# A four-layer graph network kernel: merged weights between the steps of layer 2, node weights of layer 3 summed by TensorE, one square root per pair's layer norm

## The chip, the cores and the metric

The kernel runs on one core of a Trainium2 chip, alone. The metric is the device time of one execution in microseconds (us). Each kernel was run several times, with a mean granted TensorE clock of 0.95 of full speed. In the views of the profile PE is TensorE's products, PEld its weight loads, DVE VectorE, ACT ScalarE, POOL GpSimd and SP the engine that issues loads. They count instructions, and an fp32 product is two. In the code `sb.tile` makes the tiles that engines work from and `ps.tile` those in PSUM, into which products are written; `bufs` is how many buffers a tag has.

## The reference

Eight graphs of 2048 nodes with 64 features go through four residual layers, each `x = x + layer(relu(layer_norm(x)))`. The change touches the last two:

```python
# layer 2, v = relu(layer_norm(x)) with node 0 replaced by an intervention value
for _ in range(3):
    effects = jnp.einsum('nm,bmd->bnd', adj_matrix, v)
    h = jnp.concatenate([v, effects], axis=-1)
    h = jax.nn.relu(jnp.einsum('bnk,dk->bnd', h, W1) + b1)
    v = jnp.einsum('bnk,dk->bnd', h, W2) + b2

# layer 3, x = relu(layer_norm(x)); embedding is (2048, 16), weight (16, 3, 64, 64), bias (16, 64)
w = jnp.einsum('nd,dkio->nkio', embedding, weight)
b = jnp.einsum('nd,do->no', embedding, bias)
As = [eye, A, 2.0 * (A @ A) - eye]
x_g = jnp.einsum('knm,bmc->bnkc', jnp.stack(As, 0), x)
out = jnp.einsum('bnki,nkio->bno', x_g, w) + b
```

## The kernel before

Everything is fp32. `x` lies transposed, one tile per pair of graphs, with (graph, feature) on the 128 partitions and the nodes along the free axis. A pair is worked off in four chunks of 512 nodes (`CW`); four pairs run one after another. A multiplication by the adjacency ("spread") of one chunk is sixteen products of 128 rows.

```python
def layer_norm_relu(dst, src, ps, sb, c, ...):      # one chunk
    mm(mean, avg, src[:, s], start=True, stop=True)
    nc.vector.tensor_sub(xc, src[:, s], mean)
    nc.scalar.activation(q, xc, AF.Square)
    mm(var, avg, q, start=True, stop=True)
    nc.scalar.activation(q, var, AF.Sqrt, bias=eps)
    nc.vector.reciprocal(q, q)                      # 128 x 512, of which two rows differ
    nc.vector.scalar_tensor_tensor(dst[:, s], xc, 0.0, q, op0=OP.max, op1=OP.mult)

for p in range(NP):                                  # a pair of graphs
    nc.sync.dma_start(out=xp, in_=x2_dram[p])
    ...                                              # layer norm and transposes into vN
    for step in range(3):                            # layer 2
        for c in range(NCW):
            pe = spread(vN, c)
            nc.vector.tensor_copy(ef, pe)
            mm(ph, W1v, v[:, cols(c)], start=True, stop=False)
            mm(ph, W1e, ef, start=False, stop=True)
            nc.scalar.activation(hh, ph, AF.Relu, bias=b1)
            mm(pv, W2, hh, start=True, stop=True)
            ...                                      # last: add to xp; else v = pv + b2, four transposes
    ...                                              # layer 3: layer norm, transposes, first spread y1
    for c in range(NCW):
        ...                                          # second spread y2
        for k in range(4):                           # node tiles of 128
            nc.tensor.transpose(px, xp[:, ns], ident)
            for h in range(2):                       # graphs
                for kk, src in enumerate((z[:, ns], y1[:, ns], y2[:, k * P : (k + 1) * P])):
                    for w in range(2):
                        mm(uf[:, cols(w)], src[half(h), :], W3[half(h), kk, cols(w)], ...)
                nc.vector.tensor_tensor(pr, u, emb[:, i, :, None].to_broadcast([P, D3, F]), op=OP.mult)
                nc.vector.tensor_reduce(oo, pr.rearrange("p d o -> p o d"), AX.X, OP.add)
                nc.vector.tensor_add(oo, oo, bias3[:, i, :])
                nc.vector.tensor_add(oo, oo, px[:, half(h)])
```

## Time and profile before

| | before |
|---|---|
| time, median of 4 runs | 6355.57 us (6353.63 to 6357.78) |
| busy, TensorE / VectorE / ScalarE | 86% / 66% / 40% of the span |
| layers 2 and 3 begin at | about 4212 us |
| one pair, layers 2 and 3 | 516 us |

### The profile page before, as it was taken

The numbers are of one execution on the slowest core, as the hardware profiler recorded it, in microseconds if no ns is written. First come the engines' busy times: TensorE is split into PE (matmuls) and PEld (weight loads), VectorE is DVE, ScalarE is ACT, GpSimd is POOL, SyncE is SP. The second block draws the span as 40 slices with busy tenths as digits, with TensorE's granted clock in tenths as the row PEclk, the third lists the DMA queues.
The fourth block names the chain that finished last, engine by engine and source line by source line (L and its number), as shares of the span: only waits on it lengthen the run. The fifth ranks groups of instructions, "written<-read, shape, count | busy, mean of one in ns | idle before, by whom it ended". The sixth has DMA issues, their size and how long they took to land.

```text
span 6355.8 us, 40025 instructions
## 1 busy us (share of the span) xinstructions
PE 5490.6 (86%) x15272; PEld 2629.2 (41%) x15272; DVE 4224.4 (66%) x4499; ACT 2559.2 (40%) x2656; POOL 87.0 (1%) x134
## 2 busy tenths in 40 slices
PE   5985888888888888888778888849999999999999
PEld 2433333333333333333356666634343343444444
DVE  5016999999999999999599999941153144135035
ACT  1003767676767676766266666620000000000000
POOL 0000000000000000000000000000000000000000
PEclk7996999999999999999699999979999999999999
DMA  0110000000000000000000000030000000000000
GB/s 27 66 50 0 0 0 1 0 0 0 0 0 0 0 1 0 0 0 0 1 36 31 6 30 25 5 128 0 0 5 8 0 4 10 0 2 12 0 0 7
DMA packets 44832, 73.36 MB, mean 12 GB/s; under 512 B 25296, under 2 KB 29520, under 8 KB 39760
## 3 DMA queue, kind: packets, MB, share of 16 engines
q1 hardware_dynamic: 43488, 62.41, 3.0%
q10 hardware_dynamic: 1152, 8.39, 0.3%
q8 instruction: 120, 1.97, 0.1%
q14 instruction: 72, 0.59, 0.0%
HBM read 62.40 MB, written 8.39 MB: 11 GB/s over the span
## 4 chain that ended last, share of the span: by engine, by line
DVE 45%; PE 44%; issue 6%; ACT 5%; DMA 1%; SPq 0%; ACTq 0%; DVEq 0%
PE pe L536 17%; DVE hd L315 9%; DVE hd L333 9%; DVE hd L332 9%; PE u L600 9%; PE acc L204 4%; DVE z L432 3%; DVE q L102 2%; DVE z L442 2%; PE acc L335 2%; DVE pT L456 2%; DVE z L430 2%; PE var L100 1%; PE o L459 1%; PE tp L110 1%
## 5 line engine op out<-in xcount | busy, mean ns | idle before, releaser
L335 PE MATMUL acc<-hd,sel 128*128 128x512 f32 x2048 | 1044.0, 634 | 319.1 <-DVE hd L333 318.8
L330 PE MATMUL cr<-coefT,pick 128*128 128x512 f32 x2048 | 957.7, 592 | 0.0
L314 ACT ACTIVATE hd<-h,AGm 128x1024 f32<-128x1024 f32 x512 | 586.8, 1149 | 520.0 <-PE acc L335 487.0
L335 PEld LDWEIGHTS acc<-hd,sel 128*128 128x128 f32 x2048 | 359.4, 195 | 998.8 <-DVE hd L333 737.6
L536 PE MATMUL pe<-aT,vN 128*128 128x512 f32 x1536 | 682.1, 594 | 0.0
L315 DVE SCALAR_TENSOR_TENSOR hd<-th,hd 128x1024 f32<-128x1024 f32 x512 | 651.4, 1275 | 44.5 <-ACT hd L314 31.8
L332 DVE SCALAR_TENSOR_TENSOR hd<-hd,AG,th 128x1024 f32<-128x1024 f32 x512 | 658.6, 1291 | 0.0
L459 PE MATMUL o<-pT,hN 128*128 128x256 f32 x2048 | 529.7, 395 | 114.5 <-DVE pT L456 110.9
L333 DVE TENSOR_TENSOR hd<-hd,cr 128x1024 f32<-128x1024 f32 x512 | 620.6, 1212 | 4.8 <-PE cr L330 3.9
L313 ACT ACTIVATE th<-hg,AE 128x1024 f32<-128x1024 f32 x512 | 576.6, 1135 | 42.7 <-DVE hd L332 27.9
L330 PEld LDWEIGHTS cr<-coefT,pick 128*128 128x128 f32 x2048 | 388.2, 190 | 492.4 <-issue 484.5
L331 ACT ACTIVATE th<-th 128x1024 f32<-128x1024 f32 x512 | 532.0, 1042 | 82.3 <-DVE th L316 82.0
L459 PEld LDWEIGHTS o<-pT,hN 128*128 128x128 f32 x2048 | 369.2, 192 | 211.0 <-DVE pT L456 146.2
L600 PE MATMUL u<-W,y 64*128 64x512 f32 x1024 | 450.3, 590 | 0.0
L536 PEld LDWEIGHTS pe<-aT,vN 128*128 128x128 f32 x1536 | 290.5, 191 | 353.5 <-issue 353.5
L98 ACT ACTIVATE q<-xc 128x512 f32<-128x512 f32 x64 | 40.3, 630 | 902.7 <-DVE xc L96 902.7
L556 DVE COPY ef<-pe 128x512 f32<-128x512 f32 x48 | 33.2, 692 | 548.9 <-PE pe L536 548.9
L316 DVE TENSOR_SCALAR th<-hd,AG 128x1024 f32<-128x1024 f32 x512 | 380.4, 746 | 0.6
L454 PE MATMUL tp<-ident,z 128*128 128x128 f32 x2048 | 301.9, 276 | 45.3 <-ACT pT L456 35.6
L561 ACT ACTIVATE hh<-ph,b 128x512 f32<-128x512 f32 x48 | 33.0, 687 | 707.7 <-PE ph L559 707.7
L440 ACT ACTIVATE z<-z,mx 128x2048 f32<-128x2048 f32 x128 | 256.8, 2006 | 122.9 <-DVE mx L435 122.2
L454 PEld LDWEIGHTS tp<-ident,z 128*128 128x128 f32 x2048 | 244.9, 141 | 133.2 <-ACT pT L456 86.3
(198 smaller groups left out, 5849.9 us busy)
## 6 DMA issues: line engine op xcount, KB each, us to landing
at<-in_adjT SPq DMA_DIRECT2D x16, 1024.0 KB, 5.1
neg<-in_adj SPq DMA_DIRECT2D x16, 1024.0 KB, 4.9
aT<-in_adjT SPq DMA_DIRECT2D x8, 1024.0 KB, 19.9
aT<-in_adjT ACTq DMA_DIRECT2D x8, 1024.0 KB, 19.5
x<-in_xT SPq DMA_DIRECT2D x16, 256.0 KB, 5.7
x_dram<-x SPq DMA_DIRECT2D x32, 128.0 KB, 1.9
xp<-x_dram SPq DMA_DIRECT2D x4, 1024.0 KB, 4.8
out<-ot SPq DMA_DIRECT2D x32, 128.0 KB, 1.9
```

The lines of the kernel that those rows point to most:

```text
L313: nc.scalar.activation(th, hg, AF.Tanh, bias=AE[:, b, ep : ep + 1], scale=0.5)
L314: nc.scalar.activation(hd, h2, AF.Identity, bias=AGm[:, b, ep : ep + 1], scale=0.5)
L315: nc.vector.scalar_tensor_tensor(hd, th, 1.0, hd, op0=OP.add, op1=OP.mult)
L330: mm(cr[:, cols(k)], pick, coefT[:, p, c0 + k * CW : c0 + (k + 1) * CW], start=True, stop=True)
L331: nc.scalar.activation(th, th, AF.Exp)
L332: nc.vector.scalar_tensor_tensor(hd, hd, AG1[:, b, ep : ep + 1], th, op0=OP.add, op1=OP.max)
L333: nc.vector.tensor_mul(hd, hd, cr)
L335: mm(acc[:, cols(k)], sel[b2], hd[:, cols(k)], start=b2 == 0 and ep == 0, stop=b2 == 1 and ep == 31,)
L454: nc.tensor.transpose(tp[:, w, k, :], zs[k][:, m * P : (m + 1) * P], ident)
L459: mm(o, hN[:, m, p, :], pT[:, w, :], start=m == 0, stop=m == NT - 1)
L536: mm(pe, vN[:, m, :], aT[m][:, cols(c)], start=m == 0, stop=m == NT - 1)
L600: mm(uf[:, cols(w)], src[half(h), :], W3[half(h), kk, cols(w)], start=kk == 0, stop=kk == 2,)
```

## The change

Three independent ideas, to take work from TensorE's small products and from VectorE:

- **Merged weights.** Between two steps of layer 2, `W2` and the next step's `W1` are multiplied once beforehand (`V12`, `E12`, and the biases they bring). The copy of the spread, two products and an activation per chunk disappear, and the transposes become products with `E12` that leave the result transposed.
- **One square root per layer norm.** The variances of all four chunks go into one tile, one chunk per 32 partitions, so that one `Sqrt` and one reciprocal serve the pair in place of four. A product with `spr` spreads the result out again.
- **Node weights on the partitions.** The products of layer 3 put (two embedding dimensions, 64 outputs) on the partitions and the nodes on the free axis. VectorE multiplies by the embedding, loaded in broadcast, in one instruction per graph, and TensorE sums over the dimensions with `sum2`, two stacked identities. The reductions over 16 strided elements disappear.

The core of the diff, cut (new biases, loads and tile shapes left out):

```diff
+    def layer_norm_pair(dst, src):
+        for c in range(NCW):
+            mm(pxc, cen, src[:, s], start=True, stop=True)
+            nc.scalar.activation(q, pxc, AF.Square)
+            nc.vector.tensor_scalar_max(dst[:, s], pxc, 0.0)
+            mm(var[32 * c : 32 * c + 32, :], avr, q, start=True, stop=True)
+        nc.scalar.activation(rs, var, AF.Sqrt, bias=eps)
+        nc.vector.reciprocal(rs, rs)
+        for c in range(NCW):
+            mm(pb, spr[qd, :], rs[qd, :], start=True, stop=True)
+            nc.vector.tensor_mul(dst[:, s], dst[:, s], pb)
...
-                pe = spread(vN, c)
-                nc.vector.tensor_copy(ef, pe)
-                mm(ph, W1v, v[:, cols(c)], start=True, stop=False)
-                mm(ph, W1e, ef, start=False, stop=True)
...
+                mm(pe, V12 if step else W1v, v[:, s], start=True, stop=False)
+                spread(pe, uO, c, False, True)
+                nc.scalar.activation(v[:, s], pe, AF.Relu, bias=b12 if step else b1)
+                if step < 2:
+                    sent(c, E12, False)      # four products, then a VectorE add of cbc
...
+            for dp in range(DP):             # 8 steps of two embedding dimensions
+                em = sb.tile([P, CW], FP, tag="em", name="em", bufs=3)
+                ...                          # two loads of one row, read 64 times each
+                for kk, src in enumerate((z[:, s], y1[:, s], y2)):
+                    for h in range(2):
+                        mm(u[h], W3[half(h), kk, dp * P : (dp + 1) * P], src[half(h), :], ...)
+                for h in range(2):
+                    nc.vector.scalar_tensor_tensor(
+                        pr[h], u[h], bias3[:, dp : dp + 1], em, op0=OP.add, op1=OP.mult)
+                for h in range(2):
+                    mm(pout[half(h), :], sum2, pr[h], start=dp == 0, stop=dp == DP - 1)
+            nc.vector.tensor_add(xo, pout, xp[:, s])
```

## The prediction

> **What bounds the kernel now.** I read the page's busy shares first, then the chain of work that ended last in order of time, then the groups by shape and the timeline of layers 2 and 3. The change touches nothing before 4212 us, where layer 1 ends, so only the last third matters. The groups from 4150 us on carry these lines (busy us, mean ns, idle before):
>
> ```profile
> L536 PE MATMUL pe<-aT,vN 128*128 128x512 f32 x1536 | 682.1, 594 | 0.0
> L600 PE MATMUL u<-W,y 64*128 64x512 f32 x1024 | 450.3, 590 | 0.0
> L607 DVE TENSOR_REDUCE ot<-pr 128x64 f32<-128x1024 f32 x128 | 243.2, 1900 | 4.3
> L605 DVE TENSOR_TENSOR pr<-u,emb 128x1024 f32<-128x1024 f32 x128 | 156.3, 1221 | 153.2 <-PE u L600 153.2
> L102 DVE RECIPROCAL q<-q 128x512 f32<-128x512 f32 x32 | 107.3, 3353 | 82.2 <-ACT q L101 82.2
> ```
>
> An fp32 product is two instructions: 1536 is 2 x 4 pairs x 3 steps x 64. TensorE hardly waits (third column); VectorE waits for u. So layer 3's VectorE work (1221 + 1900 + 225 + 221 = 3567 ns per u, 32 per pair, 114 us of a pair's 516) lies beside TensorE and its removal frees nothing. The chain in order of time gives one pair's length and the cost of a u block:
>
> ```profile
> 5348.88 9.44 PE pe L536 x22
> ...
> 5363.57 12.02 PE pe L536 x28
> 5380.84 12.02 PE pe L536 x28
> ...
> 5671.80 8.89 PE u L600 x24
> 5680.69 13.93 PE pe L536 x32
> ...
> 5865.81 9.44 PE pe L536 x22
> ```
>
> A pair lasts 5865.3 - 5348.9 = 516 us after correction for the different start. A 16-tile spread (32 instructions) runs one instruction per 0.43 us, 13.73 us; a chunk of a step that is not the last takes 17.33 us (5380.84 - 5363.57, and so on), of the last 16.75. So 3.6 or 3.0 us per chunk are small products and waits. A u block of one node tile takes 9.15 us for 24 instructions, less than 24 x 0.43 = 10.3. TensorE's timeline says why:
>
> ```profile
> 5141.19 0.69 PE L600 MATMUL u<-W,z 64*128 64x512 f32 x1
> 5141.61 0.59 PE L600 MATMUL u<-W,y 64*128 64x512 f32 x1
> 5141.72 0.59 PE L600 MATMUL u<-W,z 64*128 64x512 f32 x1
> 5142.04 0.59 PE L600 MATMUL u<-W,y 64*128 64x512 f32 x1
> 5142.15 0.59 PE L600 MATMUL u<-W,z 64*128 64x512 f32 x1
> ```
>
> Here the last four products of one graph (partitions 0 to 63) run beside the first four of the other (64 to 127): two 64-row streams, each at 0.43 us. Today that happens only where h changes, 4 of 24 instructions.
>
> The layer norms are the only long idle time of TensorE. Before layer 2 the timeline goes from the end of u at 5315.9 to undisturbed spreading at 5348.7, with 10 spread instructions (4.3 us) done inside: 28.6 us lost. Before layer 3, from the end of spreading at 5546.9 to 5580.7, less 6.1 us of early u and spread and 3.0 us of the chunk's own products: 24.7 us lost. Four reciprocals in each, 13.4 us, are the largest piece. The matmuls in there often take twice as long (a pair of instructions 1.92 us in place of 1.02).
>
> **What the Trainium skill says.** "TensorEngine Tiling (Array Packing)", Key Properties: different tiles run in parallel, and a change of tiling mode drains the engine. The trace agrees with both: the interleaved starts above; and from u through the 128-row transpose px back to u about 0.35 us are lost over the 0.43 grid. The same page, PSUM Bottleneck, says that tiling does not speed up evacuation; that is what my estimate of layer 3 turns on. "TensorE: Matmul & The Clock Gate", Part 1, has a half-rate clock after an idle window of about 3.4 us and full rate after as long a busy one; the doubled durations inside the layer norms agree. The same page, Part 3, says matmuls start strictly in order; here z starts before y instructions that stand ahead of it in the program, so the trace differs and I go by the trace.
>
> **The change, part by part.**
>
> *Merged weights (layer 2).* A chunk loses the copy of pe, the product with W1e, W2 and its activation, and four transposes. It keeps one product with V12 (0.86), the spread (13.73), and gains four 128-wide products with E12. The similar four with W_ind in layer 0 took 1.05 to 1.49 us, I take 1.2. In the built order the next chunk's V12 product (0.86) stands between the spread and those four, and they need Relu: about 0.2 + 0.69 + 0.06 = 0.95, so 0.1 is left as a wait. Sum 15.9 against 17.33: 1.4 x 8 chunks = 11.5 us a pair. The last step's chunk: 0.86 + 13.73 + W2 0.86 + 0.15 = 15.6 against 16.75: 4.6 us. Together 16 a pair, 64 in all.
>
> *One sqrt per layer norm.* Before layer 3: four centring and four variance products, interleaved with Square, about 8 us from the last spread; sqrt and reciprocal 0.2 + 0.69 + 3.35 + 0.1 = 4.3; then four products that copy the scale out, two PSUM buffers, against VectorE multiplies of 0.69: 4 to 6 us, half clock after 4 us of idleness; four transposes and a copy 1.5. About 19 lost, against 24.7: 5 to 7 us a pair, 26 in all. The reciprocals save 10 us, but the four chunks no longer overlap and all end behind one barrier. Before layer 2 two things eat that up. xp has one buffer, and in the old kernel its last reader was a transpose some 9 us before u ended, so its load (5 us) was hidden. Now the last reader is the final addition to xo, after the last product: 0.9 + 0.1 + 4.8 = 6 us with TensorE idle and then slow. And the sixteen W1e products (5 us) come before the first spread. I get 6 + 9 (partly at half clock) + 4.4 + 10 = 29.5 against 28.6: nothing won at three pair changes; 5 us for the first pair, whose load was exposed already. The start of layers 2 and 3 loses the wait for the late bias load (TensorE waited until 4271.5, xp landed at 4283.6): 9 us.
>
> *Node weights on the partitions (layer 3).* A chunk had 4 x 9.15 = 36.6 us of u. Now it has 8 steps of six 64-row products, alternating between the halves, and two sum2 products over 128 rows. Alternating, the six take 6 x 0.86 / 2 = 2.6 us by the interleaving above. Then a new chain sets the step: the second half's u is complete 0.17 us after its last pass; VectorE's addition and multiplication is of the form of xp<-pv,b2c,xp, 750 ns; handovers 0.1; only then can the second sum2 product (0.86) run, the first being done by about that time (its own start also waits for VectorE). With 0.1 for exposed weight loads and 0.2 to 0.3 for mode changes, a step is 2.6 + 0.17 + 0.75 + 0.1 + 0.86 + 0.3 = 4.8 us. The built order puts only one product of the next step ahead of the sums, counted in the six. 8 x 4.8 = 38.4, plus 1.3 for the chunk's first extra product, the wait for xo and the transposes: 39.7 against 36.6, 3.1 x 16 chunks = 50 us more. VectorE (1.5 us a step) and the em loads (256 KB a step against 1 MB in 4.8 us, three buffers ahead) keep up. So the part that takes the most work off VectorE slows the path.
>
> Sum: 6356.6 - 64 - 26 - 5 + 3 - 9 + 50 = 6306; I put 6302, since the last step's estimate of waits is on the cautious side.
>
> **Rivals.**
> *No overlap of the 64-row streams in the new order:* the six products take 5.15 us; the waits then partly hide, a step is about 6.9 us, 57 a chunk: +330, 6600. Against it speaks the interleaving; for it, that today's runs are of four of one kind, and that the new order switches rows every two instructions.
> *The em loads become the bound:* each is one row read 64 times and written to 64 partitions. If a step's two took over 5 us, steps would follow them: at 6 us, 8 x 1.2 x 16 = +150, 6450. A 128 KB transfer lands in 1.9 us in this trace, so I give it one in ten.
> *VectorE was the real bound and the step is shorter:* if the sums of the two halves (different columns of the array) overlap and the wait for VectorE hides, a step is 4 us, -100 more, 6200. The last dependence (u complete, 0.75, sum 0.86) doesn't allow it as the order stands: 2.6 + 1.0 + 0.86 is a floor of 4.45.
> *Clock:* with fewer and longer gaps the layer norms may run more at half clock: up to +3 us each, +24.
>
> **Range and chances.** Layer 2's gain is read off measured chunks (55 to 72); the norms and the start could give 20 to 60; layer 3 lies between +5 (steps of 4.45) and +100 (5.2), with a tail to +330. That makes 6235 to 6400. Faster by 2% is below 6229 and needs everything at its best: 0.07. Slower by 2% is above 6484 and needs one of the first two rivals: 0.13.
>
> **What would show it right or wrong.** Right: chunks of layer 2 some 15.9 us apart; u products in alternating starts and eight groups of about 4.8 us per chunk, sum2 products waiting for pr from VectorE; one 3.35 us reciprocal per norm with TensorE idle beside it; TensorE waiting for the DMA of xp at three pair changes; VectorE's busy time down by about 350 us (63 a pair in layer 3, 19 in the norms, 5 in layer 2) with no gain from the first of these. Wrong: u products one after another 0.43 us apart throughout (first rival), pr waiting for em (second), or steps below 4.4 us.

## More of the kernel before

VectorE's 66% hides two different regimes: it is busy in layers 0 and 1, which the change does not touch, and waits for TensorE afterwards. So the last third is read by itself. The next lines are the view of busy time by stretches of the kernel before, for one pair. The stretches are, in order: the steps of layer 2; the layer norm before layer 3; the first spread of layer 3; its second spread with the node weights; the change to the next pair. The columns are start and end, length, then busy us and instructions of TensorE, its weight loads, VectorE, ScalarE and GpSimd, then the granted TensorE clock, DMA share and GB/s.

```profile
5348.70:5546.90 198.20, 198.20 (x475) 84.27 (x474) 15.39 (x22) 13.64 (x20) 0.00 (x0) 1.00 0.00 0
5546.90:5580.70 33.80, 22.06 (x58) 9.11 (x57) 19.65 (x14) 7.71 (x12) 0.00 (x0) 0.90 0.00 0
5580.70:5647.50 66.80, 66.76 (x168) 29.67 (x167) 2.77 (x4) 2.93 (x5) 0.00 (x0) 1.00 0.00 0
5647.50:5832.00 184.50, 184.50 (x490) 82.70 (x489) 112.18 (x129) 0.00 (x0) 0.00 (x0) 1.00 0.04 10
5832.00:5864.90 32.90, 20.55 (x38) 8.56 (x37) 21.61 (x17) 7.03 (x11) 0.00 (x0) 0.69 0.04 8
```

In three of the five stretches TensorE is busy throughout. In the fourth VectorE works 112 of 184 us without holding anything up. TensorE idles only in the two norms, where its clock also falls, to 0.90 and 0.69.

## The result, and the profile after

| | before | after |
|---|---|---|
| median of 4 runs | 6355.57 us | 6304.95 us (6301.44 to 6308.38) |
| ratio | | 0.9921, 95% interval 0.9907 to 0.9935 |
| busy, TensorE / VectorE | 5490.6 / 4224.4 us | 5482.1 / 3879.8 us |
| one pair | 516.2 us | 506.6 us |

A ratio is the mean time of one kernel's runs over that of the other's of the same rounds, so it is not quite the ratio of the medians quoted beside it. Differences between two changed kernels below are differences of such ratios to the kernel before, times 6354 us; the interval of one ratio is 8 to 11 us either way.

VectorE lost 345 us of work and the kernel gained 51. The same stretches of the kernel after, in the same view and columns:

```profile
4808.10:4995.40 187.30, 187.30 (x479) 85.05 (x479) 8.48 (x12) 7.56 (x11) 0.00 (x0) 1.00 0.00 0
4995.40:5019.30 23.90, 18.97 (x45) 7.15 (x44) 9.35 (x10) 5.52 (x9) 0.00 (x0) 0.77 0.00 1
5019.30:5091.90 72.60, 72.57 (x179) 31.96 (x177) 2.77 (x4) 2.93 (x5) 0.00 (x0) 0.98 0.00 0
5091.90:5284.90 193.00, 192.93 (x619) 65.99 (x618) 52.64 (x72) 1.75 (x3) 0.00 (x0) 1.00 0.17 47
5284.90:5314.70 29.80, 19.23 (x61) 9.43 (x62) 11.69 (x14) 3.66 (x6) 0.00 (x0) 0.77 0.19 53
```

The boundaries are not quite comparable, because some work of a stretch runs ahead inside the one before it. Before, 4.3 us of layer 2's spreading and 1.8 us of layer 3's second part ran ahead, and 3.0 us of products of layer 2's last chunk ran late; after, 0.9 us of layer 3's second part ran ahead and 1.1 us of layer 2 late. With those put back:

| stretch of a pair | before | after | difference | predicted |
|---|---|---|---|---|
| layer 2 | 205.5 | 188.4 | -17.1 | -16 |
| norm before layer 3 and first spread | 95.8 | 94.5 | -1.3 | -5 to -7 |
| layer 3, second part | 186.3 | 193.9 | +7.6 | +12.4 |
| norm at the pair change | 28.6 | 29.8 | +1.2 | +0.9 |
| sum | 516.2 | 506.6 | -9.6 | |

The two other pair changes in the same trace lost 31.5 and 32.2 us, 2.9 and 3.6 more than before. The first pair starts spreading at 4299.7 in place of 4312.8 (with what ran ahead put back), 13.1 us earlier (predicted 14). The first three rows four times, the three pair changes and the start make -43.2 + 7.7 - 13.1 = -48.6; the two traces differ by 50.9, and the 2.3 between them were not followed.

Three of the groups by shape of the kernel after, from 4150 us on, answer to those shown of before (columns: busy us, mean ns, then the idle time ahead with its releasers):

```profile
L660 PE MATMUL u<-y,W 64*128 64x512 f32 x1024 | 351.2, 601 | 0.0
...
L666 DVE SCALAR_TENSOR_TENSOR pr<-u,bias,em 128x512 f32<-128x512 f32 x256 | 191.2, 751 | 386.8 <-PE u L660 367.1 <-DMA em<-in_embT 9.3
...
L582 DVE RECIPROCAL rs<-rs 128x512 f32<-128x512 f32 x8 | 26.8, 3353 | 9.2 <-ACT rs L581 9.2
```

The 1024 instructions that read `y1` and `y2` keep TensorE busy for 351 us in place of 450, though each lasts as long, 601 ns against 590: more of them run side by side. (A group's busy time does not see pairs with another group: the 512 instructions that read `z` went from 247 to 266 us. The step below is the surer measure: twelve u instructions in 2.78 us, where 12 x 0.43 = 5.2 would be one after another.) VectorE waits for u, not for the loads of `em` (9.3 us in all). Eight reciprocals stand where there were 32. The timeline of one step of layer 3 after shows what fills its 4.69 us; the brackets give the idle time ahead and what ended it:

```profile
5206.86 1.59 DVE L666 SCALAR_TENSOR_TENSOR pr<-u,bias,em 128x512 f32<-128x512 f32 x2 [3.09 <-PE u L660]
...
5207.66 1.91 PE L670 MATMUL pout<-pr,sum 128*64 128x512 f32 x4
5208.50 0.19 PEld L670 LDWEIGHTS pout<-pr,sum 128*64 128x64 f32 x2 [0.65 <-DVE pr L666]
...
5209.51 0.69 PE L660 MATMUL u<-z,W 64*128 64x512 f32 x1
```

VectorE makes both `pr` one after the other, from 5206.86 to 5208.45. The weights of the second sum load at 5208.50, as soon as the second `pr` is there. The two sums write different columns of the array and could run together, yet they take 1.91 us, nearly two products of 0.86 in a row. VectorE works 1.59 of the 4.69 us: it is in the chain, and is not the bound.

TensorE's timeline of the norm before layer 3 after, from the end of the one reciprocal to the first spreading:

```profile
5008.21 1.87 PE L586 MATMUL pb<-rs,spr 32*128 32x512 f32 x4 [4.16 <-DVE rs L582]
5010.85 2.67 PE L586 MATMUL pb<-rs,spr 32*128 32x512 f32 x4 [0.77 <-DVE z L587]
5013.45 1.97 PE L110 MATMUL tp<-ident,z 128*128 128x128 f32 x8
5015.35 2.07 PE L660 MATMUL u<-z,W 64*128 64x512 f32 x2
5017.35 1.97 PE L110 MATMUL tp<-ident,z 128*128 128x128 f32 x8
5019.11 3.38 PE L592 MATMUL pe<-aT,zN 128*128 128x512 f32 x4
```

After 4.16 us of idleness these pieces take about twice their usual time: the two u instructions 2.07 us, where two such instructions in m_hout take 1.05, and four spread instructions 3.38 where 4 x 0.43 = 1.7 is usual. The granted clock from 5013.45 to 5019.31 is 0.50. And all sixteen transposes stand ahead of the first spread, since the four chunks of the norm end together.

### The profile page after: what moved, and what is told of

It reads as the page before. It is cut to its first block, busy times and chain, and to the rows that moved or that the text cites. A ratio compares the mean times of both kernels' runs of the same rounds, so it can differ in the third digit from the quotient of the medians.

```text
span 6304.9 us, 41599 instructions
## 1 busy us (share of the span) xinstructions
PE 5482.1 (87%) x15856; PEld 2569.3 (41%) x15856; DVE 3879.8 (62%) x4224; ACT 2519.8 (40%) x2600; POOL 87.0 (1%) x134
## 5 line engine op out<-in xcount | busy, mean ns | idle before, releaser
L592 PE MATMUL pe<-aT,uN 128*128 128x512 f32 x1536 | 667.1, 593 | 0.0
L592 PEld LDWEIGHTS pe<-aT,uN 128*128 128x128 f32 x1536 | 289.9, 190 | 351.5 <-issue 351.5
L666 DVE SCALAR_TENSOR_TENSOR pr<-u,bias,em 128x512 f32<-128x512 f32 x256 | 191.2, 751 | 386.8 <-PE u L660 367.1
L660 PE MATMUL u<-y,W 64*128 64x512 f32 x1024 | 351.2, 601 | 0.0
L624 ACT ACTIVATE v<-pe,b 128x512 f32<-128x512 f32 x48 | 33.0, 687 | 777.8 <-PE pe L592 777.8
L610 DVE TENSOR_TENSOR uN<-pu,cbc 128x512 f32<-128x512 f32 x32 | 22.1, 692 | 483.7 <-PE pu L606 483.7
```

The lines of the kernel that those rows point to most:

```text
L592: mm(pe, vN[:, m, :], aT[m][:, cols(c)], start=start and m == 0, stop=stop and m == NT - 1)
L660: mm(u[h], W3[half(h), kk, dp * P : (dp + 1) * P], src[half(h), :], start=kk == 0, stop=kk == 2,)
```

## The experiments

The names are those of the sections. "before +" builds on the kernel before, "after +" on the changed one. All twelve kernels gave correct results. In m_lag and in the four kernels whose names begin with b_, the SBUF tiles `rs` and `ot` also have one buffer in place of two; the cuts below leave that out.

### p_l2: before + merged weights alone

```diff
-                pe = spread(vN, c)
...
+                mm(pe, V12 if step else W1v, v[:, s], start=True, stop=False)
+                spread(pe, uO, c, False)
+                nc.scalar.activation(v[:, s], pe, AF.Relu, bias=b12 if step else b1)
+                if step < 2: sent(c, E12, False)
```

> The kernel before with the merged weights of layer 2 alone (the steps keep their own layer norms and layer 3 is the old one). My theory (the parts of the sum, as the trace of the changed kernel gives them): a chunk falls from 17.33 to 15.7 us and the last step's from 16.75 to 15.7, 17 us a pair, so about 68 less, 6288; the sixteen products with W1e take some 2 us a pair more than the transposes did, which leaves 6290 to 6298. Rival (the gain of the whole change comes from the layer norms and layer 2's small products were hidden anyway): within 15 us of before.

Measured 6288.53 us, ratio 0.9898 (0.9885 to 0.9912): -65 us. The chain of work that ended last, in order of time (start, us, what), in p_l2:

```profile
5359.34 13.73 PE pe L562 x32
...
5375.01 13.74 PE pe L562 x32
```

Chunks of layer 2 stand 15.67 us apart in place of 17.33. This part did what was predicted. The time is 1.5 us below the range expected for this run: the `W1e` products cost nothing more than the transposes did (28.6 us lost at a pair change, as before), since here they lie between the norms of the single chunks.

### p_ln: before + one square root alone

```diff
-            layer_norm_relu(v, xp, ps, sb, c, ("ca", "cb"))
+        layer_norm_pair(v, xp)
...
-            layer_norm_relu(z, xp, ps, sb, c, ("ca", "cb"))
+        layer_norm_pair(z, xp)
```

> The kernel before with one sqrt and one reciprocal per layer norm alone. By the traces the norm before layer 3 costs as much as it did (the lost time there fell by 1 to 3 us a pair, not by the 6 that I had put), and the norm before layer 2, with the load of xp hidden as before, should win 5 to 6 us a pair: in all about 25 less, 6331 (6320 to 6345). Rival (the 24 reciprocals of 3.35 us that go are all on the path): 80 less, 6276. Second rival (the barrier and the half clock eat everything): within 8 us of before.

Measured 6325.09 us, ratio 0.9957 (0.9943 to 0.9970): -27 us. The reading that each of the 24 reciprocals removed was on the path (24 x 3.35 = 80 us) falls.

### p_l3: before + the new layer 3 alone

The loop over `dp` of the change, with its loads and its bias, in the kernel before:

```diff
-            for k in range(4):
-                nc.tensor.transpose(px, xp[:, ns], ident)
...
+            for dp in range(DP):
+                ...
+                    mm(pout[half(h), :], sum2, pr[h], start=dp == 0, stop=dp == DP - 1)
```

> The kernel before with the new layer 3 alone. My theory: a chunk grows by about 2 us (a step is 4.69 us in the trace, 8 of them and 1 us against 36.6), 8 us a pair, and the load of xp comes to lie open at three pair changes, 5.5 us each, while the start gains 9: 30 + 16 - 9 = 37 more, 6394 (6375 to 6410). Rival (the work taken from VectorE, 63 us a pair, is worth something on the path): faster than before.

Measured 6379.22 us, ratio 1.0039 (1.0027 to 1.0052): +25 us. The new layer 3 is slower by itself, so the part that takes the most work from VectorE costs time. It costs less than expected.

### u_l3: after + the old layer 3

The reverse edit of p_l3, on the kernel after; `var` moves to the PSUM tag `tp`.

```diff
-            for dp in range(DP):
...
+            for k in range(4):
+                nc.tensor.transpose(px, xp[:, ns], ident)
```

> The changed kernel with the old layer 3 put back (merged weights and one sqrt stay). If the parts add up, this is the changed kernel less what layer 3 cost it: 6305 - 37 = 6268 (6255 to 6285), faster than both. Rival (the new layer 3 is neutral or helps, for instance because its work joins the layer norms better): 6305 or more.

Measured 6271.92 us, ratio 0.9871 (0.9857 to 0.9884): -82 us against before and some 32 us better than after. Leaving a third of the change out beats the change.

The parts do not quite add up: alone they are worth -65, -27 and +25, together -67, and the whole is worth -50. Of the missing 17 us, 10 lie between the first two parts (-92 as a sum, -82 together in u_l3). The traces offer one candidate: at the four pairs' starts the sixteen `W1e` products take 6.6, 5.3, 6.4 and 6.7 us in u_l3, mostly at a low clock (0.51 to 0.74), where p_ln's sixteen transposes take 3.5 to 3.9 us in the same place; over four pairs that is 10 us. In p_l2 the same products lay between the chunks' norms, and one norm for the pair puts them all behind its end. This was not tested by itself, and with some 8 us either way on each ratio the rest stays open.

### m_lag: after + sums one step late

`TensorE` gets the sums of a step after the products of the next, so that both `pr` are long there.

```diff
-                for h in range(2):
-                    mm(pout[half(h), :], sum2, pr[h], start=dp == 0, stop=dp == DP - 1)
+                if dp:
+                    sums(late, dp - 1)       # the same two products, for the step before
+                late = pr                    # pr has 4 buffers in place of 2
+            sums(late, DP - 1)
```

> The changed kernel with the sums of a step issued one step late (four pr buffers), so that their operands have been ready for microseconds when TensorE comes to them. My prediction had the chain u, VectorE, sum as what sets the step. If it does, a step falls below 4.69 us: with the two sums side by side in different columns of the array 3.8 us, about 115 less in all; one after another 4.5, 25 less. The other reading of the trace (first sum starts 0.16 us after the last u pass, the wait and TensorE's own work end together): TensorE's own work sets it, nothing overlaps, within 10 us of 6305.

Measured 6210.36 us, ratio 0.9775 (0.9760 to 0.9790): -93 us against after. The chain of work that ended last, in order of time (start, us, what), in m_lag:

```profile
5209.22 1.01 PE pout L655 x4
5210.23 2.78 PE u L665 x12
```

The u products take 2.78 us as before. The sums fell from 1.91 to 1.01 us without one instruction less: with both operands ready, the two column halves run side by side. The step is 3.79 us. So the wait for the second `pr` set the step, as predicted, and a reading in which TensorE's own work is the bound falls. The saving of 7 steps x 0.9 us x 16 chunks = 101 us (the last sums of a chunk still wait) agrees with 93.

### m_hout: after + u products grouped by graph

```diff
-                for kk, src in enumerate((z[:, s], y1[:, s], y2)):
-                    for h in range(2):
+                for h in range(2):
+                    for kk, src in enumerate((z[:, s], y1[:, s], y2)):
```

> The changed kernel with the three products of one half ahead of the three of the other, in place of alternating. If the overlap needs the halves to alternate closely, only part of the six products overlaps and a step grows: overlap of four instructions saves 4 of 12 passes, so the six take 8 x 0.43 = 3.4 in place of 2.6 us: 0.8 x 128 = 100 more, 6405. Rival (TensorE finds the other half's products however they stand): within 15 us of 6305. Second rival (no overlap at all this way): 2.6 x 128 = 330 more.

Measured 6461.52 us, ratio 1.0172 (1.0155 to 1.0189): +159 us against after. The same view of m_hout:

```profile
5205.48 1.04 PE pout L670 x2
5206.53 1.05 PE u L660 x2
5207.58 1.00 PE pout L670 x2
5208.58 2.78 PE u L660 x10
```

A step is 5.89 us, and 1.2 us more in 128 steps is 154. That is some 60 us more than the theory had. Its overlap is there: of each graph's six u instructions four pair up. But each sum now stands alone, 1.0 us, with two u instructions between the two that run alone too. The product order is worth more than the whole change. Which rows a product takes, and what stands next to it, decides whether it costs 0.86 us or half of that.

### m_xp4: after + the next pair's x loaded chunk by chunk

```diff
+    xp = sb.tile([P, N], FP, tag="xp", name="xp", bufs=1)   # once, ahead of the loop
-        nc.sync.dma_start(out=xp, in_=x2_dram[p])
...
             nc.vector.tensor_add(xo, pout, xp[:, s])
+            if p + 1 < NP:
+                nc.sync.dma_start(out=xp[:, s], in_=x2_dram[p + 1, :, s])
```

> The changed kernel with one xp tile for all pairs, whose chunks for the next pair are loaded as soon as the residual addition of that chunk has read them, so three quarters of the load lie beside layer 3. Theory: TensorE's wait for this load, 5 us at each of three pair changes, goes, apart from the last chunk's, and the clock stays up: 12 to 25 less, 6280 to 6293. Rival (the time shifts to the half clock and the last chunk's load): within 8 us.

Measured 6279.83 us, ratio 0.9885 (0.9870 to 0.9900): -23 us against after. The chain of the kernel after at a pair change:

```profile
4777.29 5.79 DMA xp<-x_dram
...
4783.12 3.70 PE pxc L575 x4
```

And that of m_xp4:

```profile
5271.18 1.06 PE pxc L575 x2
5272.24 1.01 PE pout L672 x4
```

The transfer is gone, and centring products of the next pair (`pxc`) run between the last u products and the last sums. So the wait for `xp` was real, 5.5 to 6.0 us at each of three pair changes.

### m_warm: after + four unread products during the reciprocal

```diff
         nc.vector.reciprocal(rs, rs)
+        for _ in range(4):
+            idle = ps.tile([P, CW], FP, tag="tp", name="idle")
+            mm(idle, cen, q, start=True, stop=True)
```

> The changed kernel with four products whose results nobody reads, on TensorE between the variance products and the wait for the reciprocal (3.4 us of the 4.2 that it stands idle there). Theory (the half clock after that idle time is part of what ate the gain of the layer norms): with TensorE kept busy the four products that copy the scale out, the sixteen with W1e (6.3 us before the slow ones of the pairs, 5.3 before the fast one) and the first spread instructions run at full rate: 2 to 4 us less at each of eight norms, 16 to 32 in all, 6273 to 6289. Rival (what ate it is the barrier alone, a chain of single waits in which the clock doesn't matter): within 8 us of 6305.

Measured 6290.57 us, ratio 0.9904 (0.9887 to 0.9920), -11 us against after: smaller than expected, and no larger than the two intervals allow for, so the time alone would not decide it. The chain of m_warm at a norm before layer 3, to be set against the timeline of the same place in the kernel after, does:

```profile
5000.34 1.18 PE pb L589 x4
...
5002.23 1.72 PE pb L589 x4
5003.95 1.02 PE tp L110 x8
5004.98 1.05 PE u L663 x2
```

Eight transposes take 1.02 us and the two u instructions 1.05, where the same view of the kernel after has 1.90 and 2.00. The granted clock over this piece is 1.00 in place of 0.50. So the doubled durations are the clock. But the full clock held at only two of the eight norms. Of the four before layer 3 it held at this one alone: at the other three the same piece took 5.66 us again, at a clock of 0.50. And the sixteen `W1e` products took 3.99 us at one pair's start and 5.47 to 5.78 at the three others. Why these differ was not settled; the products cover 3.70 of the 4.24 us until the first `pb`, and the rest, with the waits around it, seems to be enough at times.

### b_acc: after + sums of pr on VectorE

```diff
+                    if dp:
+                        nc.vector.tensor_add(sm[h], sm[h], pr[h])
+                    else:
+                        sm.append(pr[h])
-                for h in range(2):
-                    mm(pout[half(h), :], sum2, pr[h], start=dp == 0, stop=dp == DP - 1)
+            for h in range(2):
+                mm(pout[half(h), :], sum2, sm[h], start=True, stop=True)
```

> The changed kernel with the steps of a chunk summed by VectorE (one addition of 128 x 512 per half and step, about 0.68 us) and only one pair of sum products at the end of a chunk. Theory (layer 3 is bound by TensorE, VectorE has room: 1.5 of 4.69 us): a step becomes the larger of 2.6 us of TensorE and 2 x (0.75 + 0.69) = 2.9 of VectorE, about 1.7 us less for 112 of 128 steps: 190 to 220 less, 6085 to 6115. Rival (three u buffers and VectorE's additions in front of the next release make TensorE wait): 4 us or more a step, 80 less or nothing.

Measured 6118.41 us, ratio 0.9632 (0.9617 to 0.9646): -184 us against after, 3 us above the expected range. With no sums between them, the 96 u instructions of a chunk form one piece:

```profile
5082.13 23.50 PE u L661 x96
```

A step is 23.50 / 8 = 2.94 us, where 12 x 0.43 / 2 = 2.6 is possible. VectorE is busy 19.5 of the 23.5 us; from the second step on it has no gap, and its four instructions a step take 2.84 us. I took VectorE for the bound of this step. b_gpx shows that this was only half of it.

### b_gpx: b_acc + half of the sums on GpSimd, and the loads of m_xp4

```diff
-                        nc.vector.tensor_add(sm[h], sm[h], pr[h])
+                        (nc.gpsimd if h else nc.vector).tensor_add(sm[h], sm[h], pr[h])
```

> The steps of a chunk summed on the chip's elementwise engines, one half's additions on VectorE and the other half's on GpSimd, with xp loaded chunk by chunk. With VectorE at 2.2 us a step, TensorE's 2.6 to 2.8 is the bound if GpSimd adds 128 x 512 in under that: 0.2 to 0.3 less than the 2.94 us that VectorE alone took, 30 us, and 25 from the load: 6065. Rival (GpSimd takes over 3 us for one addition, or slows VectorE beside it): at or above 6118.

Measured 6098.10 us, ratio 0.9599 (0.9585 to 0.9614): -21 us against b_acc, which is what m_xp4's loads alone are worth. The piece of 96 u instructions still takes 23.50 us, although VectorE's busy time in it fell from 19.5 to 15.5. The timeline shows who waits for whom:

```profile
5084.58 0.75 DVE L669 SCALAR_TENSOR_TENSOR pr<-u,bias,em 128x512 f32<-128x512 f32 x1 [0.70 <-PE u L663]
...
5085.38 0.18 PEld L663 LDWEIGHTS u<-z,W 64*128 64x128 f32 x1 [0.82 <-DVE pr L669]
```

VectorE idles 0.70 us for u, and then TensorE's next weights wait for VectorE to be done with `pr`, since u has three buffers and a step needs two. Two engines wait for each other in turn, and neither is the bound; from one first `pr` to the next pass 2.84 us. In b_acc two limits thus had the same length by chance, VectorE's own work and this exchange of buffers, and GpSimd took away only the first. The cure would be a fourth buffer.

### b_accxw: b_acc + the loads of m_xp4 + the products of m_warm

> All that helped so far in one kernel: merged weights, one sqrt, sums on VectorE, xp chunk by chunk, TensorE kept busy during the reciprocal. If the gains add: 6118 - 25 - (what the idle products win, 16 to 32) = 6061 to 6077. Rival (the gains of the load and of the clock are the same microseconds, since a shorter wait also keeps the clock up): 6085 to 6095.

The edit is that of the three kernels together. Measured 6085.01 us, ratio 0.9576 (0.9563 to 0.9589): in the rival's range. Against b_acc it is -36 us, and m_xp4 and m_warm gave -23 and -11 each by itself, so the gains added up; it was m_warm that had been taken too high.

### b_u4: b_gpx + the products of m_warm, with four buffers for u

```diff
-        var = ps.tile([P, CW], FP, tag="pout", name="var", bufs=1)
+        var = ps.tile([P, CW], FP, tag="tp", name="var")
...
-                u = [ps.tile([P, CW], FP, tag="u", name="u", bufs=3) for _ in range(2)]
+                u = [ps.tile([P, CW], FP, tag="u", name="u", bufs=4) for _ in range(2)]
...
+            pout = ps.tile([P, CW], FP, tag="tp", name="pout")     # only when the sums come
```

> The kernel with sums on VectorE and GpSimd, xp chunk by chunk and TensorE kept busy during the reciprocal, and with a fourth PSUM bank for u (the chunk's sum and the variances use another tile's bank). In the trace of the kernel with GpSimd a step takes 2.84 us and every one of them has TensorE's weight load waiting for VectorE to free a u bank, VectorE itself being idle 0.7 us. Theory (the three banks set the step): 2.6 us a step, 0.25 x 128 = 30 less, and some 14 from the idle products: 6045 to 6060. Rival (VectorE or GpSimd set it): a step stays at 2.8 or more, 6080 to 6090.

Measured 6046.65 us, ratio 0.9520 (0.9507 to 0.9533): 5% faster than the kernel before and 4% faster than the one after. The same piece of the chain:

```profile
5050.58 20.85 PE u L665 x96
```

A step is 2.61 us, the 12 x 0.43 / 2 that the paired streams allow. The buffer was the wait that b_gpx had left: 0.33 us x 128 steps = 42 us, and with m_warm's 11 that is about the 50 us that b_u4 gained on b_gpx. No run has the fourth buffer alone, and none adds it to b_acc, where VectorE's 2.84 us a step would remain. This is the best version.

## Why the prediction was right or wrong

The time, 6305 against a predicted 6302, is right; that it is so close is luck, because two terms, each about 19 us off, cancel.

- **Layer 2:** right. A chunk takes 15.67 us where 15.9 was predicted, one of the last step 15.70 where 15.6 was. p_l2 alone gives the -65 us of the sum's -64.
- **The start of layers 2 and 3:** right, 13.1 us for 14.
- **The pair change:** right in its mechanism. `xp` waits for the last addition and then takes 5.5 to 6.0 us on the chain; m_xp4 removes it. "Nothing won at three pair changes" came out as 1.2 to 3.6 us lost at each.
- **The norm before layer 3:** wrong in size, 1.3 us won at the pair that was measured for 5 to 7, which is 19 us over four pairs. The working was 8 + 4.3 + 4 to 6 + 1.5. The first three terms measure 7.6, 4.2 and 5.2 us. The term that failed is "four transposes and a copy 1.5": from 5013.45 to the first spread at 5019.11 pass 5.66 us, 4.8 without the u product's usual 0.86, and the spreading that follows loses another 1.5 us (its first 34 instructions take 16.05 us for 14.6). With these the norm loses 7.6 + 4.2 + 5.2 + 4.8 + 1.5 = 23.3 us, against 24.7 before. m_warm, at the norm where it kept the full clock, needs 3.0 us for the piece of 5.66, and its spreading starts at 0.43 us per instruction; at its three other norms, at a clock of 0.50, it needs 5.66. So the clock accounts for 2.7 + 1.5 = 4.2 of the 4.8 us by which the term was too small; the rest, by the working and not by a run of its own, is that the four chunks end behind one barrier and all sixteen transposes, not four, stand ahead of the spread. Half clock stood in the working for other pieces, but for this one only among the rivals, as "up to +3 us each".
- **Layer 3:** the mechanism is right, the size was off. The step takes 4.69 us where 4.8 was predicted, waits for the second `pr`, and contains paired u products. All the same it cost 7.6 us per pair for 12.4, 19 us less in all. Two terms were too large. The step is 0.11 us shorter in 32 steps of a pair, 3.5 us. And the 1.3 us at a chunk's ends measure 0.6 (a chunk without its spread takes 38.1 us, and eight steps 37.5), 2.9 us per pair: in three chunks of four the last sums stand behind spread products of the next chunk, find both `pr` ready, and take 1.01 us in place of 1.91. Together that is more than the 4.8 us missing; the rest goes the other way, mostly because the kernel before had run eight of its first u instructions early, inside the norm. The "0.35 us lost" at a transpose, which the prediction put down to changes of mode, includes the transpose's own 0.11. p_l3 alone gives +25 us, again less than expected.
- **The rivals:** no overlap of the 64-row streams falls (u products in pairs, 2.78 us for twelve instructions). What the prediction calls the last four products of a graph, running beside the next graph's, are instructions, thus two products. The `em` loads as the bound fall (9.3 us of waits in all). VectorE as the bound falls for this kernel: it works 1.59 of each 4.69 us and waits for u the rest. But the third rival was near something true. Its step of 4 us, with the sums of the two halves overlapping, is what m_lag got, 3.79 us; "as the order stands" was the condition that the experiment took away.

VectorE's busy time fell by 345 us, predicted 350, and the largest part of it came with a loss.

## What to carry to other kernels

Work taken from an engine that waits buys nothing, and if its replacement puts that engine into a chain with the busy one, it costs. Look in the timeline at what a product stands next to and whether both its operands are ready: giving the sums one step of delay was worth 93 us here, a wrong order of the same products 159 us. When two engines each seem to wait for the other, count the buffers between them before calling either the bound; and an engine without a gap may hide a second limit just as long.

## What the Trainium skill lacked or had wrong

- "TensorE: Matmul & The Clock Gate", Part 3, has matmuls start and end strictly in program order. Here products of the other 64 rows start ahead of ones that were issued earlier, in the kernel before at 5141.19 and 5141.72 us. The window it gives, 64 deep, is for weight loads; how far ahead TensorE looks among products it does not say: grouped by graph, four of a graph's six instructions pair up and the step takes 5.89 us, alternating 4.69.
- "TensorEngine Tiling (Array Packing)", Key Properties, lets tiles run in parallel. The runs agree for rows and for columns, two 64-column sums in 1.01 us. What is lacking is the condition that the second one's operand must be there in time: waiting for it, the same two take 1.91 us.
- "TensorE: Matmul & The Clock Gate", Part 1, gives an idle window of about 3.4 us for the half-rate clock. A gap of 4.16 us agrees. What share of a window must be busy to keep full rate is not said: 3.70 busy us in 4.24 kept it at two of eight norms (`W1e` products in 3.99 us) and not at the others (5.47 to 5.78 us).
- No page gives a duration for VectorE's reciprocal: 3353 ns for 128 x 512 fp32 elements, where a copy of the same shape takes 692 ns.
- "GPSIMD Engine Reference", section 3.1, has its fp32 add 1.96 times slower than VectorE's at 2048 elements. Here it is 1265 against 691 ns, 1.83 times, at 512 elements per partition: no fault, only a second size.
